# Graph attention on one core: 1642 targets instead of 106 by gathered slots

## The chip, the cores and the metric

The kernel runs on one core of a Trainium2 chip: TensorE (PE, with PEld for its weight loads), VectorE (DVE), ScalarE (ACT), GpSimd (POOL), SyncE (SP), and 16 DMA engines. The metric is the device time of one execution in microseconds, as the median of several runs.

## The reference, cut to what matters

Four layers of a graph network run over 6250 nodes and 206250 edges (100000 in both directions and one loop for each node; sorted by target). After each layer x becomes the layernorm of x plus what the layer gives. The change touches the last one, graph attention with 4 heads of 32 channels:

```
h = (x @ W).reshape(N, H, C)
a_src = jnp.sum(h * att_src, axis=-1)
a_dst = jnp.sum(h * att_dst, axis=-1)
logits = a_src[src] + a_dst[dst]
logits = jnp.where(logits > 0, logits, NEG_SLOPE * logits)
e = jnp.exp(logits - seg_max[dst])
alpha = e / (denom[dst] + EPS)
out = jax.ops.segment_sum(h[src] * alpha[:, :, None], dst, num_segments=N)
out = layernorm(out + bias) * gamma + beta
x = layernorm(x + relu(out))
```

`src` and `dst` are the edges followed by one more loop for each node. So a target's sum runs over its edges, 33 on average, and itself.

## The kernel before, in words

Nodes lie in 49 blocks of 128 (`NB`; the last holds 106), blocks in 13 `groups` of up to four. x stays in on-chip memory as `xn`. There are four stages in time: `dense0` (layer 0; it also builds the adjacency matrix in DRAM, `adj`, as edge counts in bf16), `mlp` (layer 1, edge by edge, with gathers on POOL), `dense2` (layer 2, by `adj`), and `attend` (layer 3).

`attend` has two ways to sum over the edges of a target.

**By matrices.** This serves targets in `units` of two groups, 1024 targets, six units (L1205). For each head and each unit there are 25 *steps* of two source blocks (L1438). A step loads a piece of `adj` (`load`, L1409: two blocks of sources, 1024 B runs, in a ring of four tiles `A`, three loads ahead); ACT makes for each source block a mask `r`, enormous where a_src + a_dst is positive and 0 elsewhere (L1448); DVE takes `B` = min(A, r), the counts of the edges with a positive logit (L1454), and `C` = A - B for the rest (L1456); PE multiplies both by tables of exp-weighted rows of h and adds up in PSUM (`s`, L1469, five products to a group of targets). The weights factor because exp(a_src + a_dst) is a product. `tables` makes the next head's tables during a head, in bf16 parts; `targets` spreads the next unit's a_dst over the partitions; `close` takes a finished unit out of PSUM, folds its parts and divides; in the last head it queues `finish3` for each group: bias, layernorm, gain, relu, then `update`, which adds x from `xn`, normalizes and writes back to `xn`, from where `store` sends the rows to the output. These side jobs are generators in `Lane`s: after each step each lane runs its first job on to the next `yield`, at least two steps after the last. One lane (`ends`) runs all `finish3` jobs, one after another.

**By slots.** This serves `rest`, the last group: one block of 106 targets (L123). During `dense0`, `sort` (L886) writes for each such block a list of 64 slots a target (`S`): the source of each edge, and a mark for slots that are not the target's own; such a slot's source is written as 0 (L896). In `attend`, `gathered` (L1321) takes a block in eight *chunks* of `Q` = 8 slots. A chunk is eight indirect DMAs issued by POOL (`gather`, L134), each fetching for 128 targets one row of the table `t3` in DRAM. A row has `HW` = 132 numbers, 528 B: h of the node and its a_src for four heads. DVE then forms the logit (L1363 to L1365), ACT takes Exp (L1367), DVE multiplies the rows (L1370), PE sums them into `sg` by eight fp32 products with the identity (L1373). Three chunks are issued ahead, in a ring of four tiles `g3`. The generator runs in a lane of its own with a lag of one step, from step 8 of the first unit.

The order of the instructions on each engine is the order in which the program writes them (`tc.manual_schedule()`, L114); waits between engines follow from the tiles. All loads of `adj`, the slot lists and the stores share SP's queue.

Of the kernel before, what the change touches and what calls it, by code (L numbers as in the profile page):

```python
# [9 lines left out]
F32 = mybir.dt.float32  # L10
# [8 lines left out]
P = 128  # L19
# [49 lines left out]
def kernel(  # L69
# [47 lines left out]
    HW = D + HEADS  # L117
    t1 = dram.tile([N, H], F32)
    t2 = dram.tile([N, D], F32)
    t3 = dram.tile([N, HW], F32)  # L120

    UNITS = max(1, (len(groups) - 1) // 2)
    rest = groups[2 * UNITS :]  # L123
# [378 lines left out]
    def node2(acc, al, pool, pps, n0, rows, nb, G=4, hT=None):  # L502
# [14 lines left out]
        xb = yield from update(pool, po, n0, rows, nb, m, G)  # L517
        xT = yield from transposed(pool, pps, xb, rows, nb, "xT", G)
# [16 lines left out]
        if keep:  # L535
            for c, of in ((slice(0, D), hs), (slice(D, HW), al[:, 0, b0 : b0 + nb, :])):
                nc.sync.dma_start(t3[n0 : n0 + n, c].rearrange("(b p) d -> p b d", p=rows), of[:rows, :nb])
        else:
            nc.vector.tensor_copy(hs[:rows, :nb, D:], al[:rows, 0, b0 : b0 + nb, :])
            store(t3, hs, n0, rows, nb)  # L540
# [85 lines left out]
    def finish3(po, pool, n0, rows, nb):  # L626
        o = pool.tile([P, 4, D], F32, name="o")
        gb = [gbc[:rows, k : k + 1, :].to_broadcast([rows, nb, D]) for k in range(3)]
        nc.vector.tensor_add(o[:rows, :nb], po[:rows, :nb], gb[0])
        yield from layernorm(pool, o, o, rows, nb)  # L630
        nc.vector.tensor_mul(o[:rows, :nb], o[:rows, :nb], gb[1])
        nc.vector.tensor_add(o[:rows, :nb], o[:rows, :nb], gb[2])
        yield
        nc.scalar.activation(o[:rows, :nb], o[:rows, :nb], AF.Relu)
        yield
        xb = yield from update(pool, o, n0, rows, nb)
        store(out, xb, n0, rows, nb)

    def drain(g):
        for _ in g:  # L640
            pass


    def general():
        with ExitStack() as st:
# [90 lines left out]
            def rows3(ep, eps, index, node, ri):  # L736
                g = ep.tile([P, T, HW], F32, name="g3")
# [8 lines left out]
                nc.vector.tensor_add(e, g[:, :, D:], d[:, :, :HEADS])  # L746
# [21 lines left out]
    def fast():  # L768
# [55 lines left out]
        def dense0(stack):  # L824
# [21 lines left out]
            with tc.tile_pool(name="d0o", bufs=1) as one, tc.tile_pool(name="d0", bufs=1) as ep, \  # L846
# [4 lines left out]
                eye = one.tile([P, 4, P], BF16, name="eye")  # L851
                dst_e, src_e = (v.rearrange("(e o) -> e o", o=1) for v in (dst, src))
# [143 lines left out]
                for sb in range(NS + 1):  # L996
# [5 lines left out]
                    for i in range(STEPS):  # L1002
                        g = sb * STEPS + i
                        if g == 2:
                            flush_dma(nc.sync)
                            for c in range(6):
                                load_edges(c)
# [184 lines left out]
        def attend(acc, al):  # L1192
# [12 lines left out]
            units = [(groups[2 * k][0], groups[2 * k : 2 * k + 2]) for k in range(UNITS)]  # L1205
            with tc.tile_pool(name="f3c", bufs=1) as one, tc.tile_pool(name="f3", bufs=2) as ep, \
# [113 lines left out]

                def gathered():  # L1321

                    Q = 8
                    chunks = [(g, j, q) for g, (n0, rows, nb) in enumerate(rest) for j in range(nb) for q in range(0, S, Q)]
                    rows_of, slots = {}, {}

                    def issue(i):
                        if i < len(chunks):
                            g, j, q = chunks[i]
                            if q == 0:  # L1330
                                k = rest[g][0] // P + j - R0 // 2 * 2
                                slots[g, j] = [ep.tile([P, S], dt, name=name) for dt, name in ((I32, "slot"), (F32, "none"))]
                                for t, of in zip(slots[g, j], (slot_src, slot_not)):
                                    nc.sync.dma_start(t, of[k])
                            rows_of[i] = ep.tile([P, Q, HW], F32, name="g3", bufs=4)
                            for t in range(Q):
                                gather(rows_of[i][:, t, :], t3, slots[g, j][0], q + t, P)

                    for i in range(3):
                        issue(i)  # L1340
                    yield 8
                    for i, (g, j, q) in enumerate(chunks):
                        issue(i + 3)
                        n0, rows, nb = rest[g]
                        b = n0 // P + j
                        x = rows_of.pop(i)
                        e = x[:, :, D:]
                        if q == 0:
                            if j == 0:
                                go = pool.tile([P, 4, D], F32, name="go")  # L1350

# [8 lines left out]
                            ps = rps.tile([P, HW], F32, name="sg")  # L1360
                            nc.tensor.matmul(ps, ident, own, start=True, stop=False)
                            yield
# [3 lines left out]
                        yield  # L1366
                        nc.scalar.activation(e, e, AF.Exp)  # L1367
                        yield
                        xh = x[:, :, :D].rearrange("p t (h c) -> p t h c", h=HEADS)
                        nc.vector.tensor_mul(xh, xh, e.unsqueeze(3).to_broadcast([P, Q, HEADS, CH]))  # L1370
                        yield
                        for t in range(Q):
                            nc.tensor.matmul(ps, ident, x[:, t, :], start=False, stop=q + t == S - 1)  # L1373
                        yield
                        if q + Q == S:
                            rec = pool.tile([P, HEADS], F32, name="rec3")
                            nc.vector.reciprocal(rec[:rows], ps[:rows, D:])
                            nc.vector.tensor_mul(go[:rows, j].rearrange("p (h c) -> p h c", h=HEADS),
                                                 ps[:rows, :D].rearrange("p (h c) -> p h c", h=HEADS),
                                                 rec[:rows].unsqueeze(2).to_broadcast([rows, HEADS, CH]))  # L1380
                            if j == nb - 1:
                                ends.add(finish3(go, pool, n0, rows, nb))
                            yield
# [23 lines left out]
                work = [(n0, of, a) for h, n0, of in steps for a in range(0, NB, 2)]  # L1407

                def load(i):  # L1409
                    if i < len(work):  # L1410
                        n0, of, a = work[i]
                        n, sb = min(2, NB - a), n0 // (2 * P)
                        A[i] = ep.tile([P, 4, 2, 2 * P], BF16, name="A", bufs=4)
                        for k in range(-(-width(of) // (2 * P))):
                            nc.sync.dma_start(A[i][:, k, :n].rearrange("p l q -> p (l q)"),  # L1415
                                              adj[sb + k, :, a * 2 * P : (a + n) * 2 * P])

                sums, news, ends, others = Lane(), Lane(), Lane(), Lane(1)
                for i in range(3):
                    load(i)  # L1420
                drain(targets(0, *steps[0]))
                first = [tables(0, groups[k::2], True) for k in range(2)]
                others.add(gathered())
                made, i, now = 0, 0, 0
                for k, (h, n0, of) in enumerate(steps):
# [12 lines left out]
                    for b in range(0, NB, 2):  # L1438
# [4 lines left out]
                        load(i + 3)  # L1443
                        At = A.pop(i)
                        i += 1
# [26 lines left out]
                        for lane in (sums, news, ends, others):  # L1472
                            lane.step(now)
                    sums.rest()
                    sums.add(close(h, of, [[s[to][g][:M, : of[g][1] * of[g][2]] for to in range(2)] for g in range(len(of))]))
                    sums.due = now + 2
                for lane in (others, sums, news, ends):
                    lane.rest()
# [57 lines left out]
```

## Time and profile before

| | |
|---|---|
| median of 11 runs | 5415.85 us (5399.69 to 5428.68) |
| the execution profiled | 5407.61 us, its span 5405.7 us |
| `dense0`, to about 840 us | PE busy 95% from 50 to 800 us |
| `mlp`, to about 3369 us | PE busy 80%, POOL 62% from 860 to 3340 us |
| `dense2`, 3369 to 3810 us | PE busy 98%, DMA engines 52% |
| `attend`, 3810 us to the end | 1596 us |
| loads of A | 2304 of 128 KB and 96 of 64 KB in `attend` |
| slot gathers | 64, first issued at 3831.9, last at 3936.9 us |

Stages are cut by the first and last instructions of their lines. Busy shares are an engine's busy time over the stretch. A busy DMA share is the mean over the 16 engines; of two queues it says how the engines' time went to each. Engine rows of a time list give start, length, engine, line, operation, and in brackets the idle time before it and what ended that.

### The profile page before, as it was taken

How to read it: one execution, taken by the hardware profiler on the slowest of the kernel's cores; microseconds unless marked ns; L12 is line 12 of the kernel's file. 1: busy time of each engine (PE TensorE's matmuls, PEld its weight loads, DVE VectorE, ACT ScalarE, POOL GpSimd, SP SyncE). 2: the span in 40 equal slices, each digit the busy share in tenths (PEclk: the TensorE clock that was granted, in tenths of full speed). 3: DMA queues.
4: the chain of work that ended last, by engine and by line, in shares of the span. 5: the costliest groups of instructions: out<-in, count | busy, mean ns of one | idle time of the engine just before them, and what ended most of it. 6: DMA issues, size and time to landing. Idle time of an engine off the chain costs nothing. (4 is left out here: it accounts for less than half of the span.)

```text
span 5405.7 us, 85538 instructions
## 1 busy us (share of the span) xinstructions
PE 4650.3 (86%) x30684; PEld 3385.6 (63%) x30684; DVE 3078.1 (57%) x5329; ACT 2619.7 (48%) x3739; POOL 1969.5 (36%) x1926
## 2 busy tenths in 40 slices
PE   4999997787887877887877878999789999999995
PEld 3999995555555555555555555899555555556553
DVE  7888873343343333333433434222678888888998
ACT  3444442333333333333333333100479999999985
POOL 3334324666666666666666665000510000000000
PEclk9999998998889988898988988999899999999998
DMA  5333334444444444444444443545677767777774
GB/s 115 123 123 146 121 134 129 130 129 130 126 130 129 129 124 131 126 127 126 128 126 129 130 125 119 178 181 195 170 170 216 221 209 216 221 215 215 212 211 123
DMA packets 624734, 829.84 MB, mean 154 GB/s; under 512 B 150523, under 2 KB 508449, under 8 KB 620077
## 3 DMA queue, kind: packets, MB, share of 16 engines
q1 hardware_dynamic: 536189, 595.08, 35.4%
q0 software_dynamic: 87120, 228.54, 14.8%
q8 instruction: 246, 4.03, 0.3%
q14 instruction: 187, 1.53, 0.1%
q10 hardware_dynamic: 992, 0.66, 0.1%
HBM read 730.60 MB, written 93.31 MB: 152 GB/s over the span
## 5 line engine op out<-in xcount | busy, mean ns | idle before, releaser
L135 POOL DMA_INDIRECT g<-t,edges x1617 | 1574.0, 973 | 947.8 <-issue 726.1
L1133 DVE TENSOR_TENSOR g<-g,pre 128x512 f32<-128x512 f32 x882 | 546.1, 640 | 1524.9 <-remote 434.6
L1448 ACT ACTIVATE r<-ad,bias 128x1024 bf16<-128x1024 f32 x1176 | 1255.0, 1141 | 92.5 <-DVE B L1454 91.7
L1131 PE MATMUL pre<-W1s,eaT 128*128 128x256 f32 (+1 forms) x3234 | 884.8, 415 | 313.2 <-DVE g L1133 251.6
L1469 PEld LDWEIGHTS <-acc 128*99 128x99 bf16 x5856 | 734.2, 126 | 645.0 <-issue 150.0
L1469 PE MATMUL s<-B,acc 128*99 128x512 bf16 x3504 | 868.5, 382 | 97.1 <-DVE B L1454 87.2
L1131 PEld LDWEIGHTS pre<-W1s,eaT 128*128 128x128 f32 (+1 forms) x3234 | 620.5, 205 | 447.8 <-issue 198.1
L1134 ACT ACTIVATE g<-g 128x512 f32<-128x512 f32 x882 | 507.0, 594 | 800.6 <-DVE g L1133 584.7
L1454 DVE TENSOR_TENSOR B<-A,r 128x2048 bf16<-128x2048 bf16 x600 | 720.2, 1200 | 112.1 <-ACT r L1448 67.4
L1149 PE MATMUL seg<-g,oh 128*64 128x256 f32 (+1 forms) x3234 | 612.0, 428 | 15.0 <-issue 14.8
L1122 ACT COPY eaT<-tp 128x512 f32<-128x512 f32 (+1 forms) x441 | 241.7, 548 | 698.5 <-PE tp L1120 259.9
L939 ACT CAST A<-pa 128x784 bf16<-128x784 f32 x400 | 324.9, 812 | 348.5 <-PE pa L936 320.3
L822 PE MATMUL sum<-A,xs 128*128 128x256 bf16 (+1 forms) x3675 | 467.7, 273 | 0.4 <-ACT A L939 0.4
L1456 DVE TENSOR_TENSOR C<-A,B 128x1024 bf16<-128x1024 bf16 x600 | 415.2, 692 | 63.2 <-PE s L1469 0.9
L822 PE MATMUL sum<-A,acc 128*128 128x256 bf16 (+1 forms) x3675 | 409.4, 271 | 5.6 <-DMA A<-adj 5.6
L1149 PE MATMUL seg<-ea,oh 128*64 128x128 f32 (+1 forms) x3234 | 377.4, 291 | 20.6 <-issue 19.9
L1149 PEld LDWEIGHTS seg<-ea,oh 128*64 128x64 f32 (+1 forms) x3234 | 277.3, 149 | 181.8 <-issue 70.7
L822 PEld LDWEIGHTS <-acc 128*128 128x128 bf16 x3675 | 355.1, 98 | 47.2 <-issue 7.3
L936 PE MATMUL pa<-oh,oh 128*128 128x98 bf16 x3200 | 355.7, 268 | 28.0 <-ACT A L939 23.3
L822 PEld LDWEIGHTS <-xs 128*128 128x128 bf16 x3675 | 357.4, 102 | 35.5 <-issue 0.6
L1469 PE MATMUL s<-C,acc 128*99 128x512 bf16 x1200 | 359.4, 381 | 0.4 <-DMA g<-t,slot 0.2
L1469 PE MATMUL s<-A,acc 128*99 128x512 bf16 x1152 | 346.0, 382 | 0.0
(246 smaller groups left out, 4228.8 us busy)
## 6 DMA issues: line engine op xcount, KB each, us to landing
A<-adj SPq DMA_DIRECT2D x2304, 128.0 KB
ea<-in_edge_attr_dram SPq DMA_DIRECT2D x292, 256.0 KB
A<-adj SPq DMA_DIRECT2D x100, 704.0 KB
ea<-in_edge_attr_dram SPq DMA_DIRECT2D x146, 192.0 KB
g<-t,edges POOLq DMA_INDIRECT x1617
A<-adj SPq DMA_DIRECT2D x25, 320.0 KB
t<-y SPq DMA_DIRECT2D x24, 256.0 KB
A<-adj SPq DMA_DIRECT2D x96, 64.0 KB
```

The source lines that it names most:

```text
L135: nc.gpsimd.indirect_dma_start(out=to, out_offset=None, in_=table, in_offset=bass.IndirectOffsetOnAxis(ap=index[:K, t : t + 1], axis=0))
L822: nc.tensor.matmul(ps[:, :n], parts[part][:, b, :], a(b)[:, :n], start=k == 0, stop=k == 3 * NB - 1)
L936: nc.tensor.matmul(ps[:, o, q * LO : (q + 1) * LO], ohs[g][0][:, 2 * j + o, :, q], ohs[g][1][:, 2 * j + o, :, q], start=True, stop=True)
L939: nc.scalar.copy(A[sb][:, :, q0 : q0 + 2 * QI].rearrange("p k (o q) -> p k o q", q=QI), ps[:, :, : QI * LO].rearrange("p o (q k) -> p k o ...
L1131: nc.tensor.matmul(pre[:K, t, :], eaT[i][:, b + t, :K], W1s[:, 1, :], start=True, stop=True)
L1133: nc.vector.tensor_add(gb, gb, pre[:K, :n, :])
L1134: nc.scalar.activation(gb, gb, AF.Relu)
L1149: nc.tensor.matmul(ps[half : half + W, to : to + of], oh[c][:K, a + t, :], rows[i][:K, t, :], start=a + t < 2 and to == 0, stop=a + t >= T ...
L1448: nc.scalar.activation(r[:, l, :n], ad[:, :n], AF.Relu, bias=bias[:, b + l, h : h + 1], scale=BIG)
L1454: nc.vector.tensor_tensor(wide(bt), At[:, :ns, :kk, :w], wide(r), ALU.min)
L1456: nc.vector.tensor_sub(ct[:, :n].rearrange("p (s q) -> p s q", q=w), At[:, :ns, 0, :w], bt[:, 0, :n].rearrange("p (s q) -> p s q", q=w))
L1469: nc.tensor.matmul(s[to][g][:M, : c1 - c0], row, rhs(c0, c1), start=to not in begun, stop=stop)
```

## The change

Four things change together.

1. **More targets by slots.** The first 9 of the 13 groups (4608 targets) go by matrices, in four units of two groups and one of a single group; the last four groups, 13 blocks, 1642 targets, go by slots. `sort` writes lists for these blocks too.
2. **Slots spread over the steps.** `gathered` leaves its lane. The loop counts the matrix work done (targets times source blocks) and runs the generator on so that its `3 * len(chunks)` parts lie evenly over 96% of all steps, from the eighth step on. Within it, the products of a chunk come one part later than before (`add(i - 1)`), ahead of the next chunk's DVE work and of the gathers that reuse its tile, and a block's division (`end`) after that. The first three chunks are issued before the first `targets`.
3. **Rows of 640 B.** `t3` gets 28 more columns (`HP`). They are set to 0 by two DMAs early in `dense0`, and each gather fetches them.
4. **A in x's place.** `dense2` also stores x to DRAM (`t4`). `attend` uses `xn`'s memory as a ring of three tiles for A, each of four source blocks (2048 B runs), two loads ahead. `finish3` reads its rows of x from `t4` into `was` at its start, adds them, and stores from `o`, which gets two buffers.

The diff, cut to its core:

```diff
+    HP = HW + 28
-    t3 = dram.tile([N, HW], F32)
-    UNITS = max(1, (len(groups) - 1) // 2)
-    rest = groups[2 * UNITS :]
+    t3 = dram.tile([N, HP], F32)
+    t4 = dram.tile([N, D], F32)
+    MATRIX = max(1, 9 * len(groups) // 13)
+    rest = groups[MATRIX:]
@@ node2
         xb = yield from update(pool, po, n0, rows, nb, m, G)
+        store(t4, xb, n0, rows, nb)
@@ finish3
-        o = pool.tile([P, 4, D], F32, name="o")
+        was = pool.tile([P, 4, D], F32, name="was")
+        nc.sync.dma_start(was[:rows, :nb], t4[n0 : n0 + rows * nb].rearrange("(b p) d -> p b d", p=rows))
+        o = pool.tile([P, 4, D], F32, name="o", bufs=2)
...
-        xb = yield from update(pool, o, n0, rows, nb)
-        store(out, xb, n0, rows, nb)
+        t = pool.tile([P, 4, D], F32, name="res")
+        nc.vector.tensor_add(t[:rows, :nb], o[:rows, :nb], was[:rows, :nb])
+        yield from layernorm(pool, t, o, rows, nb)
+        store(out, o, n0, rows, nb)
@@ dense0
+                rim = one.tile([P, HP - HW], F32, name="rim")
+                nc.gpsimd.memset(rim, 0.0)
...
                         if g == 2:
                             flush_dma(nc.sync)
+                            for n0, rows, nb in ((0, P, N // P), (N // P * P, N % P, 1)):
+                                if rows and nb:
+                                    nc.sync.dma_start(t3[n0 : n0 + rows * nb, HW:].rearrange("(b p) d -> p b d", p=rows),
+                                                      rim[:rows].unsqueeze(1).to_broadcast([rows, nb, HP - HW]))
@@ attend
-            units = [(groups[2 * k][0], groups[2 * k : 2 * k + 2]) for k in range(UNITS)]
+            units = [(groups[k][0], groups[k : min(k + 2, MATRIX)]) for k in range(0, MATRIX, 2)]
...
+                Q, BEFORE = 8, 3
+                def issue(i):
...
+                        rows_of[i] = ep.tile([P, Q, HP], F32, name="g3", bufs=BEFORE + 1)
+                        for t in range(Q):
+                            gather(rows_of[i][:, t, :], t3, slots[g, j][0], q + t, P)
...
+                    def add(i):
+                        x, q = rows_of.pop(i), chunks[i][2]
+                        for t in range(Q):
+                            nc.tensor.matmul(ps, ident, x[:, t, :HW], start=False, stop=q + t == S - 1)
...
                     for i, (g, j, q) in enumerate(chunks):
+                        if i:
+                            add(i - 1)
+                        issue(i + BEFORE)
...
                         nc.vector.tensor_add(e, e, al[:, 1, b].unsqueeze(1).to_broadcast([P, Q, HEADS]))
                         nc.vector.scalar_tensor_tensor(e, e, SLOPE, e, op0=ALU.mult, op1=ALU.max)
                         nc.vector.tensor_sub(e, e, less[:, q : q + Q])
                         yield
+                        if i:
+                            end(i - 1)
                         nc.scalar.activation(e, e, AF.Exp)
                         yield
...
                         nc.vector.tensor_mul(xh, xh, e.unsqueeze(3).to_broadcast([P, Q, HEADS, CH]))
                         yield
...
-                work = [(n0, of, a) for h, n0, of in steps for a in range(0, NB, 2)]
+                LB = 4
+                room = xn.rearrange("p b d -> p (b d)").bitcast(BF16)
+                work = [(n0, of, a) for h, n0, of in steps for a in range(0, NB, LB)]
...
-                        n, sb = min(2, NB - a), n0 // (2 * P)
-                        A[i] = ep.tile([P, 4, 2, 2 * P], BF16, name="A", bufs=4)
+                        n, sb = min(LB, NB - a), n0 // (2 * P)
+                        ring = slice(i % 3 * 4 * LB * 2 * P, (i % 3 + 1) * 4 * LB * 2 * P)
+                        A[i] = room[:, ring].rearrange("p (k l q) -> p k l q", k=4, l=LB)
...
+                slotted, taken, gone = gathered(), 0, 0
+                parts = 3 * len(chunks)
+                every = 0.96 * (NB * sum(width(of) for h, n0, of in steps) - 8 * 4 * F) / max(1, parts)
...
-                        load(i + 3)
+                        l0 = b % LB
+                        if l0 == 0:
+                            load(i + 2)
...
+                        gone += n * kk
+                        while taken < parts and gone - 8 * 4 * F >= taken * every:
+                            next(slotted, None)
+                            taken += 1
```

`rows3` of the general path, which other inputs would take, follows the wider rows (`e` from columns `D:HW`).

## The prediction

> **What bounds the kernel now.** I read the busy shares first: POOL alone has room, and it rests in attention. Then the table by stage, then the groups by shape, for the stretch from 3400 us on:
>
> ```profile
> PE 4650.3 (86%) x30684; PEld 3385.6 (63%) x30684; DVE 3078.1 (57%) x5329; ACT 2619.7 (48%) x3739; POOL 1969.5 (36%) x1926
> ```
> ```profile
> 3810.00:3866.00 56.00, 31.48 (x187) 19.83 (x185) 39.97 (x109) 29.53 (x43) 27.72 (x22) 0.76 0.47 134
> 3866.00:3927.00 61.00, 47.18 (x230) 29.73 (x230) 47.51 (x90) 39.24 (x45) 45.84 (x36) 0.94 0.79 163
> 3927.00:5346.00 1419.00, 1349.56 (x6583) 815.19 (x6583) 1248.34 (x1812) 1273.13 (x1357) 7.91 (x8) 0.99 0.71 211
> 5346.00:5405.70 59.70, 5.54 (x38) 4.42 (x36) 41.68 (x161) 7.23 (x17) 0.00 (x0) 0.55 0.08 23
> ```
> ```profile
> L1448 ACT ACTIVATE r<-ad,bias 128x1024 bf16<-128x1024 f32 x1176 | 1255.0, 1141 | 92.5 <-DVE B L1454 91.7
> L1454 DVE TENSOR_TENSOR B<-A,r 128x2048 bf16<-128x2048 bf16 x576 | 703.7, 1222 | 111.0 <-ACT r L1448 67.4 <-DMA A<-adj 29.7 <-PE s L1469 3.6
> L1456 DVE TENSOR_TENSOR C<-A,B 128x1024 bf16<-128x1024 bf16 x600 | 415.2, 692 | 63.2 <-PE s L1469 0.9 <-DVE B L1454 0.5
> L135 POOL DMA_INDIRECT g<-t,slot x64 | 81.5, 1273 | 47.6 <-DVE acc L1262 23.4 <-issue 18.5 <-ACT r L1448 3.7
> ```
>
> Columns of the table: length, PE, PEld, DVE, ACT, POOL, clock, DMA share, GB/s. Attention is the 1596 us from 3810. In its long stretch PE is busy 95%, ACT 90%, DVE 88%, the DMA engines 71%: whatever the gathers add falls on engines that are nearly full. The chain of waits gives the cadence (start, length): one unit is 58.5 us, of 25 steps of 2.16 us on PE (ten 512-column matmuls) and some 5 us of closing.
>
> ```profile
> 4564.09 4.48 PE s L1469 x20
> ...
> 4622.61 4.48 PE s L1469 x20
> ```
>
> Last, a gather with the DVE operation in whose course it began, and the DMA queues in an early and a late 10 us of the 64 gathers (3862 to 3872, then 3922 to 3932; q0 is the gathers, q1 the loads of A):
>
> ```profile
> 3854.72 1.95 POOL L135 DMA_INDIRECT g<-t,slot  x1 [0.30 <-issue]
> ```
> ```profile
> 3854.63 1.22 DVE L1454 TENSOR_TENSOR B<-A,r 128x2048 bf16<-128x2048 bf16 x1 [0.23 <-issue]
> ```
> ```profile
> q1 hardware_dynamic: 1975, 1.79, 56.3%
> q0 software_dynamic: 225, 0.48, 19.4%
> ```
> ```profile
> q0 software_dynamic: 171, 0.37, 70.0%
> q1 hardware_dynamic: 927, 0.84, 29.9%
> ```
>
> 64 gathers are 2048 packets, 32 each. So a gather holds all 16 DMA engines for 1.94/7.0 = 0.28 us early and 7.00/5.3 = 1.31 us late. The line that makes the lists writes node 0 into each slot that a target does not use (source times mine), and targets have 33 edges for 64 slots on average (206250/6250): I read the late price as 128 reads of one DRAM row. While it lasted, the chain ran through A's loads, and steps began at 3927.5, 3933.7, 3945.3, 3953.4 and 3960.2, some 8 us apart instead of 2.4.
>
> **Removed.** 600 full-width steps become 400 full and 100 half-width ones, 450 in equivalents. 150 x 58.5/25 = 351 us go, a gain only if the rest of a step does not grow.
>
> **Added in each chunk.** The gathered blocks go from 1 to 13: 104 chunks of 8 slots, 832 gathers. The pace is 0.96 x (903168 - 16384)/312 = 2729 target-blocks a part, three parts a chunk; a full step gives 2048. So a chunk shares 4 steps with:
> - PE: 4 x 2.16 + 1.80 (16 sg records, 3884.68 to 3886.48) + 0.7 (fold matmuls and transposes, 2.2 us a group, 9 groups to 28 chunks) = 11.1 us.
> - DVE: 4 x 1.94 (B start to next B where DVE sets it) + 2.0 (four operations on a chunk, 0.19, 0.19, 0.20, 1.22, and a block's eighth) + 0.64 (closing) + 0.77 (next head's tables) = 11.2 us. In the last head the layernorms take the tables' place: 12.3.
> - ACT: 4 x 2.09 + 0.23 + 0.8 = 9.4 us.
> - POOL: in the trace, eight gathers beside four steps spanned 12.9, 12.0 and 12.1 us (from 3887.4, 3901.2, 3914.0). A gather that begins within a DVE operation with two SBUF inputs ends 0.82 us after that operation; undisturbed it takes 0.94, plus 0.30 to the next. Floor 8 x 1.25 = 10.0.
> - DMA, A: 214.5 MB took 71.3% of 1000 us, 1.74 us of all engines a step at 1024 B runs; dense2's 5632 B runs, 73.0 MB in 50.3% of 400 us, would give 1.44. Runs of 2048 B: I take 1.55, nearer the first, 6.2 a chunk (5.8 to 7.0).
> - DMA, gathers: 2.2 us for a chunk of used slots, 7.3 for the sixth (41.5% of 10 us, 146 packets, 3902 to 3912), 10.5 for the last two.
>
> **The sum.** Five chunks of a block are bound by PE and DVE: 11.2/0.94 = 11.9 us, 0.94 being DVE's share in the units from 5100 on, where both are full. POOL's 12.3 does not bind them: in the hot chunks it needs only 10 to 11 and runs ahead, as far as the ring of four. The sixth is 7.3 + 6.2 = 13.5, the last two 16.7 each, DMA-bound. A block: 59.5 + 13.5 + 33.4 = 106.4 us, thirteen 1383. To it: 56 us to the ninth step, where slots start; 25 for unit 0's tables and the last head's layernorms; 64 for the last 4% of the steps (5.4 full ones and a half-width unit that DVE fills, 51 us); the 59 us tail, whose five pending layernorms of 9.25 us stay about five. Attention 204 + 1383 = 1587 against 1596: 9 us less. The execution profiled took 5407.6, so 5399; the median of the runs lies 8 above it: 5407.
>
> **What I cost at nothing.** The 25 stores of x to DRAM: SP queues each ahead of a store that already waits longer, in a stage where PE is 98% busy and DMA 52%; uncovered, 25 x 0.37 = 9 us. The 13 reads of x: issued at a group's start, used six yields later; uncovered in the tail, at most 5 x 3. The pad: 6250 runs, at the 48 ns of A's packets 19 us of all DMA engines at about 30 us; behind it on SP stand edge lists that nothing needs before 840. It could delay the first slot searches by those 19 us, a gain I exclude. Loads into x's place: blocks 0 to 31 are free well before 3810, so 0; a slot list now waits on SP behind A's loads, with three chunks' lead, 0 to 2 us a block. The general path (`rows3`) does not run on these inputs.
>
> **A rule against the padding.** Late gathers differ from early ones by the row that they read, 1.31 against 0.28 us, at the same 528 B; so its length is not what the trace prices. The Trainium skill, "DMA: Bandwidth & Descriptors", section "How a descriptor splits into AXI transactions", says that reads go in pieces of up to 256 B from 256 B boundaries, in beats of 32 B. By it node 0's row grows from 17 beats to 20; as an estimate the hot chunks would be 10.5 x 20/17 + 6.2 = 18.6 and attention 49 us longer. No run here shows 640 B rows.
>
> **Rivals.**
> 1. The hot rows hide. The ring gives three chunks' lead and A has 4 to 8 blocks in hand; averaged over a block the DMA engines need 8 x 6.2 + 5 x 2.2 + 7.3 + 21 = 89 us, less than PE. Then all chunks take 12.0 to 12.8: attention 1452 to 1535, the median 5272 to 5355. Against it: the late gathers took 70% of the engines the moment that they were queued, and A starved.
> 2. The hot rows cost more, and the kernel is slower. If the price goes by bytes, 640/528 = 1.21: 12.7 + 6.2 = 18.9, the sixth 15.0, a block 112.3 to 114.6 (with POOL's 12.35 in the cold ones): attention 1664 to 1694, median 5484 to 5514. It decides from 107.1 us a block, that is 17.05 for a hot chunk, 1.36 us a gather; 1.31 was measured, so the margin is thin.
> 3. POOL locks to DVE. With B and C back to back each gather ends 0.82 us after a B and the next begins in the next B: one a step, as from 3852.4 to 3859.1 (2.2 us apart). Four at 2.16 and four at 1.25 give 13.6 for every chunk but the hot: a block 115, attention 1699, median 5519. For it: steadier B's than in unit 0, where the rate was measured. Against it: the chunk's own DVE work breaks the lock.
>
> **How the numbers follow.** The even case, 0.40, reaches from 5365 to 5445 (a block 103 to 109): half of it faster, a quarter within 0.2% (11 us, about what a measurement of this kernel can tell from no change), a quarter slower. Rival 1 has 0.25, rival 2 0.25 (from 5445 on), rival 3 0.10. Faster 0.20 + 0.25 = 0.45; same 0.10; slower 0.10 + 0.35 = 0.45. The range leaves out rival 1's floor and the two slow rivals' joint end: 5275 to 5525.
>
> **What would show it.** Right: about 13 rounds in attention, in each a stretch with PE near 95% and one where B waits for A's loads and the DMA share is over 0.9; q0 near 10 us of all engines in a hot chunk; POOL busy some 1100 us in attention. Wrong: PE over 93% throughout (rival 1); q0 above 12 us in a hot chunk (rival 2); B waiting for gathered rows with DMA below 0.8 (rival 3); anything over 20 us before 3810.

## The result, and the profile after

The changed kernel is slower: 5559.91 us (median of 8 runs, 5545.15 to 5574.49) against 5412.44 us beside it; ratio 1.0271, 95% interval 1.0254 to 1.0288. Forecast were 5407 us and 5275 to 5525. The execution profiled took 5554.88 us, its span 5553.0. The stages ahead of attention did not move (`dense2` ends at 3814.9 us before and 3810.0 after, by its last product); attention went from 1590.8 to 1743.0 us.

Busy shares on the page:

```profile
PE 4585.3 (83%) x30540; PEld 3405.9 (61%) x30540; DVE 2964.5 (53%) x5525; ACT 2374.9 (43%) x3637; POOL 2874.4 (52%) x2695
```

The table by stage (columns as before):

```profile
3810.00:3866.00 56.00, 29.00 (x107) 16.16 (x108) 41.19 (x113) 31.01 (x43) 31.45 (x27) 0.73 0.53 172
3866.00:3927.00 61.00, 49.77 (x247) 31.09 (x246) 48.02 (x90) 41.56 (x49) 45.26 (x36) 0.97 0.75 167
3927.00:5500.00 1573.00, 1267.70 (x6456) 823.48 (x6455) 1132.86 (x2002) 1026.73 (x1250) 912.94 (x770) 0.92 0.75 182
5500.00:5553.00 53.00, 0.00 (x0) 0.00 (x0) 35.93 (x146) 6.09 (x16) 0.00 (x0) 0.50 0.18 48
```

In the long stretch PE is busy 81% where it was 95%, DVE 72% where it was 88%; the DMA engines are at 75%. The engines have less to do, as forecast (in attention PE 1346 us against 1429, DVE 1258 against 1376, ACT 1105 against 1349). What came is idle time on every one of them. The groups by shape in attention name its main causes (lines of the matrix steps are L1485 for r, L1491 for B, L1506 for s now):

```profile
L137 POOL DMA_INDIRECT g<-t,slot x832 | 989.7, 1189 | 599.7 <-issue 291.5 <-DMA slot<-slot_src 108.6 <-ACT r L1485 50.3
L1485 ACT ACTIVATE r<-ad,bias 128x1024 bf16<-128x1024 f32 x784 | 845.2, 1137 | 270.8 <-DVE B L1491 216.7 <-issue 53.6
L1491 DVE TENSOR_TENSOR B<-xn,r 128x2048 bf16<-128x2048 bf16 x384 | 469.4, 1222 | 313.6 <-DMA xn<-adj 169.3 <-PE s L1506 53.4 <-issue 25.1
L1493 DVE TENSOR_TENSOR C<-xn,B 128x1024 bf16<-128x1024 bf16 x400 | 276.8, 692 | 57.9 <-PE s L1506 11.8 <-remote 6.6 <-PE na L1320 0.9
```

B waits 169 us for loads of A (`xn<-adj`; 29.7 before, from 3400 us on). POOL waits 109 us for slot lists. And a part ends by "issue" on ACT and DVE at once: these engines waited for nothing that the profile shows.

The time goes in rounds, one for each gathered block. By POOL's time list the first gathers of two chunks lie about 13 us apart through seven chunks of a block, then some 27 us at the last; from block to block it is 117 to 130 us. Here is one such place: the table by stage for 30 us ahead of it and 30 us in it, the two DMA queues in the latter, and there DVE's B operations that waited.

```profile
4120.00:4150.00 30.00, 27.49 (x146) 20.10 (x145) 21.85 (x37) 19.65 (x24) 15.97 (x14) 0.89 0.64 163
4150.00:4180.00 30.00, 20.14 (x85) 11.45 (x83) 17.39 (x27) 14.35 (x18) 18.81 (x16) 0.84 0.90 146
```
```profile
q0 software_dynamic: 752, 1.29, 56.6%
q1 hardware_dynamic: 1692, 3.09, 33.7%
```
```profile
4155.77 1.22 DVE L1491 TENSOR_TENSOR B<-xn,r 128x2048 bf16<-128x2048 bf16 x1 [2.58 <-DMA xn<-adj]
...
4165.17 1.23 DVE L1491 TENSOR_TENSOR B<-xn,r 128x2048 bf16<-128x2048 bf16 x1 [4.37 <-DMA xn<-adj]
...
4175.36 1.23 DVE L1491 TENSOR_TENSOR B<-xn,r 128x2048 bf16<-128x2048 bf16 x1 [4.76 <-DMA xn<-adj]
```

The gathers (q0) hold 56.6% of the engines' time there. A tile of A, two steps, arrives every 10 us, so four steps take 20 us instead of 11. The chain of waits passes through the same place. Behind it, it names the late list of the next block; B does not read that list, but the loads of A share its queue, and what releases an operation is inferred.

```profile
4159.09 16.14 DMA xn<-adj
4175.36 1.24 DVE B L1491
...
4184.21 5.64 DMA slot<-slot_src
```

Over the whole of attention the two queues are near what the sum had (698 and 511): 734 us of all engines for A with the few stores and lists in its queue, 528 us for the gathers.

```profile
q1 hardware_dynamic: 151740, 238.64, 42.1%
q0 software_dynamic: 39936, 68.21, 30.3%
```

### The profile page after: what moved, and what is told of

It is laid out like the page before. It is cut to its first block, busy times and chain, and to the rows that moved or that the text cites. A ratio compares the mean times of both kernels' runs of the same rounds, so it can differ in the third digit from the quotient of the medians.

```text
span 5553.0 us, 84777 instructions
## 1 busy us (share of the span) xinstructions
PE 4585.3 (83%) x30540; PEld 3405.9 (61%) x30540; DVE 2964.5 (53%) x5525; ACT 2374.9 (43%) x3637; POOL 2874.4 (52%) x2695
## 5 line engine op out<-in xcount | busy, mean ns | idle before, releaser
L137 POOL DMA_INDIRECT g<-t,slot x832 | 989.7, 1189 | 599.7 <-issue 291.5
L1485 ACT ACTIVATE r<-ad,bias 128x1024 bf16<-128x1024 f32 (+1 forms) x980 | 972.8, 1052 | 316.6 <-DVE B L1491 253.4
L1506 PEld LDWEIGHTS <-acc 128*99 128x99 bf16 x4392 | 577.8, 132 | 773.5 <-issue 452.4
L1506 PE MATMUL s<-B,acc 128*99 128x512 bf16 x2628 | 706.7, 404 | 319.4 <-DVE B L1491 264.8
L1491 DVE TENSOR_TENSOR B<-xn,r 128x2048 bf16<-128x2048 bf16 (+1 forms) x500 | 548.0, 1096 | 346.6 <-DMA xn<-adj 180.6
L829 PEld LDWEIGHTS <-acc 128*128 128x128 bf16 x3675 | 356.1, 99 | 53.0 <-issue 12.1
L1493 DVE TENSOR_TENSOR C<-xn,B 128x1024 bf16<-128x1024 bf16 (+1 forms) x500 | 319.4, 639 | 69.5 <-PE s L1506 11.8
L945 PEld LDWEIGHTS <-oh 128*128 128x128 bf16 x3200 | 302.9, 117 | 35.9 <-issue 21.8
```

Source lines behind the costliest of these rows:

```text
L137: nc.gpsimd.indirect_dma_start(out=to, out_offset=None, in_=table, in_offset=bass.IndirectOffsetOnAxis(ap=index[:K, t : t + 1], axis=0))
L829: nc.tensor.matmul(ps[:, :n], parts[part][:, b, :], a(b)[:, :n], start=k == 0, stop=k == 3 * NB - 1)
L945: nc.tensor.matmul(ps[:, o, q * LO : (q + 1) * LO], ohs[g][0][:, 2 * j + o, :, q], ohs[g][1][:, 2 * j + o, :, q], start=True, stop=True)
L1485: nc.scalar.activation(r[:, l, :n], ad[:, :n], AF.Relu, bias=bias[:, b + l, h : h + 1], scale=BIG)
L1491: nc.vector.tensor_tensor(wide(bt), At[:, :ns, :kk, :w], wide(r), ALU.min)
L1493: nc.vector.tensor_sub(ct[:, :n].rearrange("p (s q) -> p s q", q=w), At[:, :ns, 0, :w], bt[:, 0, :n].rearrange("p (s q) -> p s q", q=w))
```

## The experiments

One thing must be known to read them. The runs fell into two sorts: in some sets the kernel before took 5412 to 5419 us (the set of the result among them), in others 4956 to 4966 us, the difference lying in its `mlp` stage (`dense2` ends near 3815 us or near 3370 us). What sets the two sorts apart is not known; sets of both sorts bear the same chip number, 11, so nothing shows that it is the chip, as some of the expectations below assume. Each ratio below is to the kernel before in the same set, and "at 5417" or "at 4961" says which sort it was. Attention is counted from the last product of `dense2`.

### The hot row

Four of these kernels change only what the slots read; the others change the length of a row, the time of the list, or the number of groups.

`after_spread`: an unused slot keeps the source that its place in the edge list names (an edge of another target), which the mark masks as before.

```diff
-                        nc.vector.tensor_tensor(of, s, mine, ALU.mult)
-                        nc.sync.dma_start(slot_src[k0 : k0 + 2].rearrange("b p s -> p b s"), of)
+                        nc.sync.dma_start(slot_src[k0 : k0 + 2].rearrange("b p s -> p b s"), s)
```

> The changed kernel, but a slot that a target does not use keeps the source of the neighbouring edge that stands there, in place of node 0; it is masked as before, so the result is the same. Theory H (one DRAM row read over and over holds the DMA engines, and A starves): a gather costs 0.3 to 0.4 us of all DMA engines throughout, q0 in attention falls from some 528 us of all engines to 250 to 330, the bursts of 15 to 20 us in which B waits for A go, and the median falls from 5560 by 150 to 300 us, to 5260 to 5410. Theory L (POOL is the bound: it waits for a slot list at each block, and its gathers lock to DVE): the address read does not matter; within 40 us of 5560.

Measured at 4961: ratio 0.9684 (0.9668 to 0.9700), attention 1430.0 us, gathers 257 us of all DMA engines.

`before_spread`: the same edit in the kernel before.

> The kernel before with the same edit to its one gathered block. Theory H: the slow steps from 3921 to 3958 go, 20 to 30 us less: 5385 to 5395. Theory L: no change, within 10 us of 5412.

Measured at 4961: ratio 0.9948 (0.9932 to 0.9965), that is 28 us; attention 1569.6 us. So the kernel before paid for the row too, with 64 gathers.

`after_allhot`: every slot of the gathered targets reads node 0, so their sums are wrong.

```diff
-                        nc.vector.tensor_tensor(of, s, mine, ALU.mult)
+                        nc.vector.tensor_scalar(of, s, 0.0, None, op0=ALU.mult)
```

> The changed kernel with node 0 in all 64 slots of every gathered target (so the gathered rows' sums are not the reference's, and 1642 targets come out wrong). Theory H: all 832 gathers cost 1.2 to 1.4 us of all DMA engines, 1000 to 1160 us beside A's 734, so attention is bound by DMA at 1800 to 2000 us: median 5640 to 5850. Theory L: within 40 us of 5560.

Measured at 4961: ratio 1.0886 (1.0861 to 1.0910), attention 2020.2 us, gathers 931 us. The table by stage and the queues for the middle 1400 us:

```profile
3500.00:4900.00 1400.00, 1012.56 (x4908) 649.54 (x4908) 844.08 (x1462) 775.61 (x963) 714.37 (x624) 0.86 0.88 156
```
```profile
q0 software_dynamic: 29958, 51.16, 49.4%
q1 hardware_dynamic: 100936, 166.58, 38.2%
```

A read of the one row costs 931/832 = 1.12 us of all engines for 128 rows, a read of distinct rows 257/832 = 0.31. With all reads hot a chunk takes (2020 - 204)/104 = 17.5 us (204 being the start and end that the sum on record sets aside, an estimate), with none (1430 - 204)/104 = 11.8. The inputs say how many reads are hot: of the eight chunks of a block the share of unused slots is 0, 0, 1, 21, 69, 96, 100 and 100%, together 3.87 chunks. 8 x 11.8 + 3.87 x (17.5 - 11.8) = 116.5 us a block. The changed kernel at 4961 (below) took (1689.4 - 204)/13 = 114.3. So at 4961 the price of the hot reads goes by their number; they don't hide.

`after_rows16`: unused slots read rows 0 to 15, by the low four bits of the source.

```diff
+                        few = ep.tile([P, 2, S], I32, name="low")
+                        nc.vector.tensor_scalar(few, s, 15, None, op0=ALU.bitwise_and)
+                        nc.vector.tensor_tensor(few, few, none, ALU.mult)
                         nc.vector.tensor_tensor(of, s, mine, ALU.mult)
+                        nc.vector.tensor_tensor(of, of, few, ALU.add)
```

> The changed kernel with each unused slot pointing at one of rows 0 to 15 (10 KB of DRAM, by the low bits of the neighbouring source) instead of row 0; masked as before. If the price is that of one row read by all, 16 rows relieve it nearly wholly: ratio 0.965 to 0.985. If it is that of a narrow stretch of DRAM, it stays: 1.01 to 1.03.

Measured at 5417: ratio 0.9938 (0.9915 to 0.9962), attention 1567.9 us, gathers 241.5 us. Sixteen rows are as good as thousands (1570.5 us in the same set, `spread_nopad` below). What costs is that one row is read by all, not that few are.

`after_nopad` and `spread_nopad`: rows of 528 B again (`HP = HW`, no `rim`), with and without the hot row.

```diff
-    HP = HW + 28
+    HP = HW
```

> The changed kernel with rows of 528 B again (no pad, no rim). Theory bytes: node 0's row costs by its length, so 17.5% less of the unused slots' share of q0, some 50 us of q0 in attention and 30 to 60 us of time: ratio to before 1.015 to 1.021 where the changed kernel has 1.027. Theory pieces: both lengths take three pieces of 256 B, no difference, 1.024 to 1.030. Theory alignment: 528 B rows that start anywhere cost more in the used slots, ratio 1.03 to 1.05.

> Unused slots spread over other rows as in after_spread, and rows of 528 B. It prices the pad where no row is hot. Theory alignment: q0 in attention rises from 257 to 280 us or more and the ratio to before from 0.968 to 0.972 to 0.98; theory bytes: q0 falls to about 215 and the ratio to 0.960 to 0.966; theory pieces: 0.966 to 0.970.

Measured at 5417: with the hot row 1.0286 (1.0230 to 1.0342), attention 1740.4 us, gathers 550 us; without 0.9936 (0.9915 to 0.9956), 1570.5 us, 210 us. The changed kernel's rows of 640 B gave 1.0271 and, in another set, 1.0327; without the hot row 0.9947. So the padding moves the time by nothing that these runs can tell. In the distinct reads it is there, 210 to 258 us of the DMA engines (1.23, the bytes' 1.21), where they have room; in the hot reads it is not.

`after_list`, `after_third`, `list_again`: a block's slot list loaded half a block earlier, once by itself, and once more beside the changed kernel.

```diff
-                        if q == 0:
-                            k = rest[g][0] // P + j - R0 // 2 * 2
+                        for c in [0] * (i == 0) + [i + S // Q // 2] * (q == S // 2):
+                            if c < len(chunks):
+                                g1, j1, q1 = chunks[c]
+                                k = rest[g1][0] // P + j1 - R0 // 2 * 2
...
```

> The changed kernel with each block's slot list loaded half a block earlier (at the fifth chunk issued of the block before), nothing else. Theory L: POOL's wait for the lists, 12 times 10 to 18 us, goes, and with it 100 to 200 us: 5360 to 5460. Theory H: the wait stood beside the DMA engines' hot stretch; at most 50 us less: 5510 to 5560.

> The changed kernel as it is, beside the next run. Beside a kernel before of 4961 us: if the late list costs nothing, attention 1711 and ratio 1.027, as with the earlier list; if it adds its wait less what the ring of three chunks covers, 30 to 90 us more, ratio 1.033 to 1.045. Beside a kernel before of 5417 us: attention 1740 to 1775, ratio 1.027 to 1.033 as before.

> The changed kernel with each block's slot list loaded half a block earlier, so that POOL's first gather of a block does not wait for it. If the wait is covered (the prediction's claim, with a larger wait): within 0.3% of the run before. If not: 30 to 90 us faster than it, ratio 0.006 to 0.017 lower; the DMA engines, full in the hot stretch, then set the pace, so the gain is less than the 109 us that POOL waited.

Measured at 4961: `after_list` 1.0266 (1.0242 to 1.0290); in the later set the changed kernel 1.0222 (1.0205 to 1.0239), with the earlier list 1.0223 (1.0206 to 1.0240). POOL's wait for lists, 62 us in `after_third`, is gone from the list of waits, and B waits for A as much as before (250 us there, 272 with the earlier list). POOL now waits for the products that free its ring (`PE sg`: 103 us, 3 before). So at 4961 the list's wait costs nothing; at 5417, where POOL waited 109 us, no run tells.

`after_m12`: 12 of 13 groups by matrices, as in the kernel before, with all else of the change (x in DRAM, four blocks to a load, spread slots, padded rows).

```diff
-    MATRIX = max(1, 9 * len(groups) // 13)
+    MATRIX = max(1, 12 * len(groups) // 13)
```

> The changed kernel with 12 of the 13 groups by matrices: again one gathered block of 106 targets, its 24 parts now spread over all steps, with the wide rows, A by four blocks and x in DRAM. If the targets moved to slots carry the loss (theory H), the rest is worth little: ratio 0.985 to 1.000, since the one block's hot chunks lie 300 us apart and find A loaded ahead. If x in DRAM or the ring of A costs (rival), 1.005 to 1.03.

Measured at 5417: 1.0019 (0.9997 to 1.0041), attention 1594.9 us. Parts 2 to 4 of the change are together worth nothing that shows; the loss comes with the 12 further blocks.

### What is left without the hot row

Without it attention took 1430 us at 4961 and 1568 to 1570 at 5417. The next runs ask why. In the table the changed kernel at 4961 is from another set than the two below it.

`spread_again`, `spread_third`: the kernel `after_spread` twice more. `spread_plain`, `plain_again`: the same, with one load of 1024 consecutive rows in the place of a chunk's eight gathers, so that the gathered targets sum wrong rows.

```diff
-                        for t in range(Q):
-                            gather(rows_of[i][:, t, :], t3, slots[g, j][0], q + t, P)
+                        o = i * 5 % 40 * P
+                        nc.sync.dma_start(rows_of[i], t3[o : o + Q * P].rearrange("(q p) d -> p q d", p=P))
```

> The changed kernel with unused slots reading distinct rows, once more, because the first run of it stood beside a kernel before of 4966 us and the later runs beside one of 5419 us. Theory I (on chips where the kernel before takes about 5415 us, all engines get their instructions late while POOL issues gathers; elsewhere they do not): beside a kernel before of 5415 us attention 1560 to 1575 us, ratio 0.993 to 0.995, and PE's idle time ended by issue over 40 us in attention; beside one of 4966 us attention about 1430, ratio 0.968. Theory II (the 640 B rows, or something else in the kernels that have been run, makes the difference, not the chip): 0.968 and attention about 1430 beside either.

> As the run before with distinct rows, but the eight gathers of a chunk are replaced by one plain load of 1024 consecutive rows, so POOL issues no gathers in attention and the same bytes arrive; the 1642 targets' values are those of wrong sources, so its output is not the reference's. Theory I (late instructions come with POOL's gathers): beside a kernel before of 5415 us attention 1400 to 1450 us, ratio 0.965 to 0.975, PE's idle time ended by issue below 10 us. Theory III (the late instructions come with the number of instructions of PE, DVE and ACT in attention, or with the DMA traffic, whoever issues it): attention stays at 1540 to 1575, ratio 0.992 to 0.996. Beside a kernel before of 4966 us nothing of it can show, and the difference to the run before is what the eight gathers of a chunk cost POOL and DVE by themselves: 0 to 30 us.

> Distinct rows for the unused slots, third time. Theory I (the chip decides): beside a kernel before of 5415 us attention 1560 to 1575, ratio 0.993 to 0.995, PE idle time ended by issue over 40 us between 3900 and 5300; beside 4965 attention 1430, ratio 0.969. Theory II (the length of the rows decides, 528 B in the runs beside 5419): ratio 0.969 beside either.

> One plain load of 1024 consecutive rows for each chunk, no gathers by POOL; the 1642 targets' values are those of wrong sources. Beside a kernel before of 4965 it took ratio 0.975 and attention 1466, 33 us more than with gathers, because a 640 KB load in A's queue delays A. Beside one of 5415: theory I (late instructions come with POOL's gathers) attention 1440 to 1480, ratio 0.970 to 0.980, and no idle time of POOL, PE and DVE ended by issue beyond that of the other chip (PE's weight loads 157 us); theory III (they come with the instructions of PE, DVE and ACT, whoever loads) attention 1560 to 1610, ratio 0.993 to 1.003.

> The changed kernel as it is, beside the next two. If the chip is one where the kernel before takes about 5415 us: ratio 1.027, attention 1740 us, q0 about 530. If it is one where it takes about 4965: attention about 1710, ratio 1.026 (from the run with the earlier list, 1.0266), so that the hot row costs 280 us there against 172 on the other, because on the other part of it lies over time that late instructions cost anyway.

Measured:

| kernel | at 4961 | at 5417 |
|---|---|---|
| changed | 1.0222, attention 1689.4 us | 1.0327 (1.0296 to 1.0357), 1771.6 us |
| distinct rows | 0.9695 (0.9678 to 0.9711), 1432.8 us | 0.9947 (0.9932 to 0.9962), 1552.2 us |
| plain loads | 0.9753 (0.9737 to 0.9769), 1468.5 us | 0.9774 (0.9746 to 0.9802), 1475 us |

(By the last product of `dense2`, `spread_plain` has 1468.5 us; the expectation of `plain_again` says 1466.) With plain loads attention takes nearly the same in both sorts. So the 119 us by which distinct rows differ come with POOL's gathers, in one sort of set. The waits of DVE, PE and ACT from 3900 to 5300 us, first `spread_third` at 5417, then `plain_again` in the same set, which has but the last of these lines (`spread_again` at 4961 too, with 0.3 us; PE's weight loads, which run ahead of it, are left out here):

```profile
PE s L1504 <- issue: 51.1, 55, 5.6
ACT r L1483 <- issue: 39.2, 40, 5.9
DVE B L1489 <- remote: 25.2, 7, 7.5
DVE B L1489 <- issue: 21.7, 26, 4.8
```
```profile
DVE B L1489 <- issue: 0.3, 1, 0.3
```

One such moment, the time list of `spread_third`:

```profile
4027.30 0.95 POOL L137 DMA_INDIRECT g<-t,slot  x1 [0.30 <-issue]
...
4028.04 0.38 PE L1504 MATMUL s<-xn,acc 128*99 128x512 bf16 x1 [1.03 <-issue]
...
4028.76 0.38 PE L1504 MATMUL s<-C,acc 128*99 128x512 bf16 x1 [0.35 <-issue]
...
4030.18 0.38 PE L1504 MATMUL s<-C,acc 128*99 128x512 bf16 x1 [1.04 <-issue]
...
4031.05 0.95 POOL L137 DMA_INDIRECT g<-t,slot  x1 [0.30 <-issue]
4034.64 1.75 SPq L1442 DMA_DIRECT2D xn<-adj  x4
4034.68 1.22 DVE L1489 TENSOR_TENSOR B<-xn,r 128x2048 bf16<-128x2048 bf16 x1 [7.45 <-remote]
4035.94 1.15 ACT L1483 ACTIVATE r<-ad,bias 128x1024 bf16<-128x1024 f32 x1 [11.43 <-DVE B L1489]
```

While POOL puts out a gather every 1.25 us, PE gets one product in 0.7 to 1.4 us; then for 2.6 us nothing runs at all. SP and DVE go on within 0.04 us of each other, and ACT right behind DVE. In the 8 us from 4027 the DMA engines are busy 22%. That the engines' instructions arrive late, as the name "late instructions" below has it, is a reading of this picture. Another is that PE alone was late, or told the others so late, since SP's load and DVE's B may both wait for its products; the profile does not name what released them. That it comes with the gathers is shown by the plain loads. Why one sort of set has it and the other does not is open.

The kernel before had shown it, in `mlp`, where POOL gathers all the time. Its waits from 860 to 3340 us, and then, from `before_spread` at 4961, the line of the same wait of POOL:

```profile
POOL g L135 <- issue: 710.3, 1395, 5.3
...
DVE g L1133 <- remote: 434.6, 77, 13.9
...
DVE g L1133 <- issue: 251.0, 90, 8.3
```
```profile
POOL g L135 <- issue: 396.6, 1302, 0.3
```

At 4961 no such wait of POOL is longer than 0.3 us (the usual gap between two gathers), and DVE's g has none of either kind; in the kernel before of the result DVE waits 686 us of that stage for "remote" and "issue", and the stage is some 450 us longer.

### How far the trade pays

`spread_q7`: only 56 of 64 slots are gathered (`SQ` is 56), which leaves out two edges of one target. `spread_m10`, `spread_m8`: ten or eight groups by matrices (the diff shows ten). All with distinct rows.

```diff
-                chunks = [(g, j, q) for g, (n0, rows, nb) in enumerate(rest) for j in range(nb) for q in range(0, S, Q)]
+                chunks = [(g, j, q) for g, (n0, rows, nb) in enumerate(rest) for j in range(nb) for q in range(0, SQ, Q)]
```
```diff
-    MATRIX = max(1, 9 * len(groups) // 13)
+    MATRIX = max(1, 10 * len(groups) // 13)
```

> Distinct rows, and only the first 56 of the 64 slots are gathered: 91 chunks instead of 104, 728 gathers instead of 832. One target has more than 56 edges and loses two of them, so its output differs from the reference in that row. Where each chunk costs its place beside four steps (11.9 us by the sum on record, 13.1 us as measured beside a kernel before of 5415), 13 chunks less do not shorten the matrix steps, they only take their own engine time: PE 13 x 2.5 us, DVE 13 x 2.7 us, or 32 to 35 us, ratio 0.006 below the run with distinct rows; if what bounds is the rate of gathers (theory I's late instructions), it is 13/104 of the time that they add (about 130 us beside 5415): 16 us more, ratio 0.009 below. If the matrix steps alone bound, nothing: within 0.002.

> Distinct rows, ten of thirteen groups by matrices instead of nine: 50 more full-width step equivalents (2.34 us each at the pace of before, 117 us) and 9 gathered blocks instead of 13. If a gathered block costs what its eight chunks add to an unloaded step stream (8 x (1.8 + 0.7) = 20 us of PE, 22 us of DVE), four blocks less give 80 to 90 us back, so 27 to 37 us slower than with nine: ratio 0.005 to 0.007 above the run with distinct rows. Where instructions come late with the gathers (theory I, 130 us for 832 gathers), 256 gathers less give 40 us more back: within 0.002 of it or faster.

> Distinct rows, eight of thirteen groups by matrices: 50 full-width step equivalents less (117 us at 2.34 us), 17 gathered blocks instead of 13 (1088 gathers, 136 chunks). Theory A (each chunk adds what it costs PE and DVE, 2.5 to 2.7 us, as from ten to nine groups, which gained 43 us): 40 us less again, ratio 0.961 beside a kernel before of 4961 us and 0.987 beside one of 5417. Theory B (POOL's gathers bound: 1.45 us from gather to gather beside the steps, 1088 of them 1580 us): attention 1500 to 1640 beside 4961, ratio 0.985 to 1.01; beside 5417, where a chunk took 13.0 us without hot rows, 136 x 13.0 + 204 = 1970, or ratio above 1.03.

Measured at 4961: q7 0.9639 (0.9623 to 0.9655), attention 1411.8 us; m10 0.9782 (0.9766 to 0.9798), 1476.2 us; m8 1.0244 (1.0227 to 1.0261), 1707.6 us. Nine groups are best. Thirteen chunks less are worth 21 us, less than the 32 to 35 us expected. From ten to nine groups 43 us are won; from nine to eight 275 are lost, more than the expectation's 1640 us of attention allowed for. Waits of `spread_m8` from 3460 to 4900 us:

```profile
ACT g L1395 <- DVE g L1391: 352.8, 77, 8.9
DVE g L1389 <- DMA g<-t,slot: 291.1, 97, 7.6
...
POOL g L137 <- issue: 263.0, 862, 0.3
```

Here the chunk waits for its rows and POOL goes from gather to gather with 0.3 us between them (its longest wait is 1.1): a chunk takes 92.6/8 = 11.6 us (from block to block on POOL's time list), the rate of the gathers themselves. At nine groups, read in the same way from `spread_again`, it is 12.1, so that the spread slots sat almost on POOL's limit.

**The version that beats both** is the change with distinct rows: 0.9684 and 0.9695 at 4961, but only 0.9947 at 5417, half a percent.

## Why the prediction was wrong

- **The first step that failed is "Five chunks of a block are bound by PE and DVE: 11.2/0.94 = 11.9 us".** For the work that it counted it was right: 11.8 us at 4961, with PE busy 94% and DVE 89% from 3500 to 4700 us in `spread_again`. In the sets at 5417 a chunk without hot rows takes 13.0 us, (1552.2 - 204)/104, or 13.1, (1570.5 - 204)/104. The sum had no term for the late instructions that come with the gathers there, 119 and 138 us of attention above the 1432.8 at 4961. The reading began at 3400 us; the sign stood in the waits of `mlp`, the stage of before with the most gathers, which the prediction did not read.
- **The second is "The sixth is 7.3 + 6.2 = 13.5, the last two 16.7 each".** It gives a block 11.2 us more than eight cold chunks. Measured are 19.7 us at 4961, (1689.4 - 1432.8)/13, and at 5417 16.9 in one set, (1771.6 - 1552.2)/13, and 13.1 in the other, (1740.4 - 1570.5)/13. By the prices of `after_allhot`, which make it 22.1 us, three sizes were off, as an estimate: the fourth and fifth chunk by 5.2 us, since 21 and 69% of their slots are unused and they were taken as cold; the sixth by 3.9, since 96% of its slots are unused; the last two by 1.8. One window of one block stood for the count that the inputs give. And the last two were taken as full DMA engines, 10.5 + 6.2. With every read hot a chunk takes 17.5 us, though it needs only 931/104 = 8.95 us of all engines for gathers and at most 766/104 = 7.4 for A: the engines' share stays at 0.88, and A's own packets grow dearer (766 against 716 us).
- **The DMA totals were nearly right, partly by luck: two errors met.** A's queue cost 733.8/450 = 1.63 us a step (1.55 taken), the gathers 40.6 us a block (39.3). The hot price was too high (1.31 against 1.12 us a gather), the count of hot reads too low. Totals in balance said nothing on where they fall.
- **The miss in the two sets at 5417 that have both kernels** is 1771.6 - 1587 = 185 us and 1740.4 - 1587 = 153 us (rows of 528 B). Of these the hot reads are 13 x (16.9 - 11.2) = 74 and 13 x (13.1 - 11.2) = 25, late instructions 119 and 138, and the cold chunk at 11.8 for 11.9 is -9. The split depends on what is counted first: with the hot reads at their price of 4961, 13 x (19.7 - 11.2) = 111 us, late instructions are 82 and 51. The two cost less together than one by one. In the execution of the result the miss was 156, and how that splits was not measured there.
- **POOL does not bind: right**, but with less room than the floor of 10.0 us said; its rate is 11.6 in `spread_m8`. A gather within a DVE operation with two SBUF inputs still ends 0.82 us behind it (4167.51 + 1.98 against 4167.45 + 1.22). Rival 3's lock, one gather a step, did not form: gathers average 1.19 us.
- **What was costed at nothing** cost nothing: the stages ahead of attention did not move, the last 53 us (59.7 before) hold the layernorms, and the change without the further blocks gives 1.0019. The wait for slot lists was mis-sized, 0 to 2 us a block against up to 19 us at a time, but at 4961 it cost nothing: 1.0222 and 1.0223.
- **The rule against the padding.** By the Trainium skill, "DMA: Bandwidth & Descriptors", section "How a descriptor splits into AXI transactions", the prediction estimated 49 us for the longer row 0. The runs with rows of 528 and 640 B show no difference (attention 1740.4 us, against 1743.0 and 1771.6). The measurement decides: the price of the hot row does not go by its beats.
- **The rivals.** The first, hot rows hide, fell: the DMA engines needed 32 x 1.63 + 40.6 = 92.8 us of a block's 118, and yet A starved, because the hot reads lie together and A has two loads in hand. The second had the direction, but neither its mechanism (bytes) nor its sign: a hot chunk's gathers cost 8.95 us, not over 12. What would show the forecast right was in fact seen, the rounds, PE at 92% in one stretch and B waiting for A at a DMA share of 0.90 in the next; only longer ones. POOL was busy 990 us instead of some 1100.

## What to carry to other kernels

Give unused slots of a gather harmless but different rows (16 are enough) and mask them; here a padding index of 0 was a hot spot, and its price is in the number of such reads, which the inputs tell. When a change multiplies an operation, read how the kernel fares in the stage where that operation is already frequent, with waits for "issue" and "remote" included, even if that stage is not touched. And where a bursty queue shares the DMA engines with a steady one, sum them burst by burst against the loads in hand, not over a period.

## What the runs showed of the hardware

- 128 reads of one 640 B row in DRAM took as much DMA time as 1.12 us of all 16 engines (`after_allhot`), of distinct rows 0.31 (`after_spread`), of 16 rows 0.29 (`after_rows16`, 241.5/832 with half the slots real).
- The price of distinct rows went with the bytes (210 and 258 us for 832 gathers of 528 and 640 B), that of the mix with the hot row did not (550 against 528 and 556 us).
- In some sets PE, DVE, ACT and SP stood still together while POOL issued gathers (DVE up to 7.5 us at a time in `spread_third`, the DMA engines 22% busy in one such moment); plain loads of the same bytes did not do it. It is worth 119 us of attention there.
- One plain load of 640 KB for each chunk in A's queue cost 36 us at 4961 against gathers on their own queue (1468.5 against 1432.8); B waited for A in 24 places, 49 us, instead of 7, 13 us.
- Gathers of 128 rows beside the matrix steps went out one in 1.45 us on average where nothing else held POOL (11.6 for eight, `spread_m8`).
